# Posts' weights rounded on Pool, a fixed order at the end with the experts' sums in four stages, and a longer search for the order of the main loop

## The chip, the cores and the metric

The kernel runs on one core of one Trainium2 chip. The metric is the device time of one execution in microseconds; lower is better. The engines are named as in the profile: PE (TensorE; PEld its weight loads), DVE (VectorE), ACT (ScalarE), POOL (GpSimd), SP (SyncE, which issues all DMAs here).

## The reference

One transformer layer in float32 on 4 sequences of 2048 tokens with 256 channels.

```python
x = x + attn(layernorm(x))          # 16 heads of 16 channels, softmax over 2048 keys,
                                    # attn(y) = heads @ w_o.T + b_o + y
y = layernorm(x)
scores = softmax(y @ w_gate.T)      # 8 experts
s = (scores + expert_bias) in 4 groups of 2: keep the 2 groups with the largest sums
topk_idx = top 2 experts of what is kept; weights = scores there
flat_idx = topk_idx.reshape(-1)     # expert numbers, 0 to 7, are used as row numbers
routed_in = y[flat_idx] * weights   # so only rows 0 to 7 of y are ever gathered
counts = bincount(topk_idx)         # rows 0..counts[0]-1 go through expert 0, and so on
h = silu(grouped(routed_in, w1)) * grouped(routed_in, w3); routed_out = grouped(h, w2)
shared = silu(y @ sw1.T) * (y @ sw3.T) @ sw2.T
out = shared.at[flat_idx].add(routed_out)   # and only rows 0 to 7 of out receive them
x = x + out
```

## The kernel before, in words

**Chunks and units.** The tokens are cut into 16 chunks of 512. A chunk gets its layernorm, its projections to q, k and v (`qkv`, or hand-woven code for the first sequence), then attention, then its post work (`post`): output projection, second layernorm, transposes (`to_channels`), routing (`route`) and the shared feed-forward (`shared`, products `pa`, `pb`, `pd`). Attention runs in 64 units: one sequence, four heads and 512 queries each. Numbers are kept as a rounded high part and a low part (`h`, `l`), and a product is three matmuls (`mm3`).

**The three streams of a unit.** "M": a score matmul `mx` of 128 queries against 512 keys and a row maximum `ms` on DVE. "S": a score matmul `st` of 128 keys against 512 queries, with the maximum subtracted as a 64th row, and an exponential `et` on ACT. "A": the value matmuls `av`, eight PE instructions for four heads. The 4096 M, 4096 S and 1024 A of the whole run share seven PSUM banks (tags `b0` to `b6`). The maxima of a unit go through `mt` and a DMA into row 63 of its `qst` before its S may start.

**The order of the main loop.** The order is written out by the program itself while it is built, and the engines PE, DVE, POOL and ACT run it as written (`manual_schedule`). `Plan` books every instruction on model clocks. At each step `refill` puts up to `HORIZON` = 46 operations (M, S, A, the copy O of a finished unit, and P and D, pieces of side work) into a window, `Ahead.search` exchanges or moves two of them at random `TURNS` times and keeps an order by its modelled cost (simulated annealing), and the first `COMMIT` operations of the result are given out. Side work comes from generators; `need(kind, ns, *tiles)` says on which engine their next piece costs what and which tiles it waits for, `gate` holds one back until a condition holds. Pieces for ACT and POOL ("a", "p") are given out as soon as the plan thinks their tiles ready.

**Places the change touches.** `setup` loads w_o, s_1, s_3 and s_2 at the start of the third unit and splits each with `split(..., eng=G)`: the high part on ACT (`S.copy`), the low part on POOL. `post_first` loads a chunk's sums of exponentials and takes their reciprocals on DVE. After the last unit, `last_heads` finishes the last four heads, and `finish` runs two generators in turn for the last chunk: `front` (`post_a`, `route`, `moe`) and `behind` (`post_b`, the shared feed-forward). In `finish` the order on the engines is left to the framework's scheduler. `moe` builds one-hot tables for the 16384 routed rows, 16 groups of 1024: `ranges` (which expert a row falls to, from the counts `m_cum`), `pick` (one-hot `ob` on DVE, squared weights `ow` on POOL, then `mo` on PE and its copy `oT`), `hidden` (matmuls `mu`, sigmoid tables `mth` on ACT and DVE) and `gather` (matmuls into `pg`). In `pick` a group's `ob`, `mo` and `oT` stand together.

Of the kernel before, what the change touches and what calls it, by code (L numbers as in the profile page):

```python
# [32 lines left out]
LEAD0 = 3  # L33
LEAD = 6
HORIZON = 46
COMMIT = 10
LATE = 0.01, 0.1, 16
TURNS = 1600
WARM = 1.5
NET = 6  # L40
BANKS = 7
# [365 lines left out]
def body(tc, B, L, cols, x, wqkv, bqk, wst, bst, bv, wo, bo, wg, w1, w2, w3, sw1, sw2, sw3, ebias, cst, pad, out):  # L407
# [21 lines left out]
    def need(kind, ns=0, *tiles, more=0, act=940):  # L429


        return kind, ns, tiles, more, act

    def gate(open_):

        return "g", open_, (), 0, 0
# [43 lines left out]
    def split(name, tmp, out=None, eng=None):  # L480

        h, l = out or [cp.tile([P, 2, tmp.shape[2]], F32R, tag=f"{name}{q}", name=f"{name}{q}") for q in "hl"]
        S.copy(h, tmp)
        (eng or V).tensor_tensor(l, tmp, h.bitcast(F32), ALU.subtract)
        return h, l

# [73 lines left out]
    def to_channels(src, name, keep=None, fast=False, out=None):  # L560

        h, l = out or hl(f"t_{name}")
        if not fast:
            for c in range(2):
                f = keep[:, c, :] if keep is not None else sb.tile([P, QC], F32, tag="qkf", name=f"f_{name}{c}", bufs=2)
                pt = stile(f"pt_{name}{c}")
                for i in range(TQ):
                    T.transpose(pt[:, i * P:(i + 1) * P], src[:, i, c * P:(c + 1) * P], ident)
                S.copy(f, pt)
                G.tensor_copy(h[:, c, :], f)  # L570
                G.tensor_tensor(l[:, c, :], f, h[:, c, :].bitcast(F32), ALU.subtract)
                if c == 0:
                    yield need("s1", 436, act=470)
            return h, l
        for c in range(2):
            pt = mtile(f"pt_{name}{c}")
            for i in range(TQ):
                T.transpose(pt[:, i * P:(i + 1) * P], src[:, i, c * P:(c + 1) * P], ident)
            S.copy(keep[:, c, :], pt)
            S.copy(h[:, c, :], pt)  # L580
            V.tensor_tensor(l[:, c, :], pt, h[:, c, :].bitcast(F32), ALU.subtract)
            yield
        return h, l

    mark = {}
# [244 lines left out]
    def moe():  # L830
# [9 lines left out]
        V.tensor_copy(tot, pc[0:E, 0:P])  # L840
        cum = mtile("m_cum")
        T.matmul(cum[:, 0:E + 1], tot, K["below"][0:E, :], start=True, stop=True)
        ge = sb.tile([P, NR, E + 1], BF16, tag="vst", name="m_ge", bufs=2)
        oe = sb.tile([P, NR, E], BF16, tag="hq", name="m_oe", bufs=2)
        gb = sb.tile([P, E, 32], F32, tag="qkf", name="m_gb", bufs=2)
# [2 lines left out]
        pg = ps_av.tile([P, QC], F32, tag="av", name="pg")  # L848
        GR = 8
        NG = NR // GR  # L850
        ows, oTs, ths = {}, {}, {}

        def ranges(r0, r1):
            n = r1 - r0
            V.tensor_tensor(ge[:, r0:r1], K["rows"][:, r0:r1].unsqueeze(2).broadcast_to([P, n, E + 1]),
                            cum[:, 0:E + 1].unsqueeze(1).broadcast_to([P, n, E + 1]), ALU.is_ge)
            V.tensor_tensor(oe[:, r0:r1], ge[:, r0:r1, 0:E], ge[:, r0:r1, 1:E + 1], ALU.subtract)

        def pick(g):
            sl = slice(g * GR, (g + 1) * GR)  # L860
            ob = sb.tile([P, GR, E, 8], BF16, tag="x", name=f"ob_{g}", bufs=2)
            ow = ows[g] = sb.tile([P, GR, E, 8], F32, tag="lo", name=f"ow_{g}", bufs=3)
            ee = oe[:, sl, :].unsqueeze(3).broadcast_to([P, GR, E, 8])
            V.tensor_tensor(ob, ee, of[:, sl, :].unsqueeze(2).broadcast_to([P, GR, E, 8]), ALU.mult)
            G.tensor_tensor(ow, ee, oj[:, sl, :].unsqueeze(2).broadcast_to([P, GR, E, 8]), ALU.mult)
            pt = mtile(f"mo_{g}")
            obf = ob.rearrange("p r e j -> p (r e j)")
            for q in range(GR // 2):
                T.matmul(pt[:, q * P:(q + 1) * P], obf[:, q * P:(q + 1) * P], identb, start=True, stop=True)
            oT = oTs[g] = sb.tile([P, GR // 2, P], F32R, tag="hi", name=f"oT_{g}", bufs=3)  # L870
            V.tensor_copy(r2(oT), pt)
# [120 lines left out]
    last = {}  # L992

    def post_last():

# [67 lines left out]
            V.tensor_tensor(xv, pd, xv, ALU.add)  # L1063
        write(ch, x1)

    def post_b(ch, n, x1, x2T, x2hl, rt, eng=G, hhl=None):

        hT = f4(f"hT_{n}")
        hhl = hhl or hl(f"hT_{n}")
        for m in range(2):  # L1070
            pa = mtile(f"pa_{n}_{m}")
            mm3(pa, W["s_1"], x2hl, slice(m * P, (m + 1) * P), slice(0, QC))
            th = sb.tile([P, QC], F32, tag="sth", name=f"th_{n}_{m}", bufs=2)
            S.activation(th, pa, AF.Tanh, scale=0.5)
            if eng is G:
                yield
            if eng is None:
                S.copy(hT[:, m, :], pa)
                G.tensor_tensor(th, th, K["ones"][:, 0:1].broadcast_to([P, QC]), ALU.add)
                G.tensor_tensor(th, th, hT[:, m, :], ALU.mult)  # L1080
            else:
                V.scalar_tensor_tensor(th, th, 1.0, pa, ALU.add, ALU.mult)
            yield
            next(rt, None)
# [3 lines left out]
            if eng is None:  # L1088
                S.mul(hT[:, m, :], pb, 0.5)
                G.tensor_tensor(hT[:, m, :], hT[:, m, :], th, ALU.mult)  # L1090
            else:
                V.scalar_tensor_tensor(hT[:, m, :], pb, 0.5, th, ALU.mult, ALU.mult)
            S.copy(hhl[0][:, m, :], hT[:, m, :])
            (eng or G).tensor_tensor(hhl[1][:, m, :], hT[:, m, :], hhl[0][:, m, :].bitcast(F32), ALU.subtract)
            yield
            next(rt, None)
            yield
        yield
        for half in range(2):
# [24 lines left out]
    def finish():  # L1124
# [12 lines left out]
        while live:  # L1137
            for g in list(live):
                try:
                    next(g)  # L1140
                except StopIteration:
                    live.remove(g)


    queue, posts, side, norms, sums, firsts = (deque() for _ in range(6))
# [272 lines left out]
    def setup():  # L1418
# [359 lines left out]
```

## Time and profile before

| | |
|---|---|
| median of 3 runs | 3067.62 us (3067.2 to 3068.33) |
| the profiled execution | 3064.53 us, span 3062.7 us |
| mean granted PE clock | 0.986 |
| busy: PE, DVE, ACT, POOL | 2982.9, 2823.3, 2420.8, 649.9 us |
| first `st`, last `mx`, last `av` starts at | 93.5, 2930.5, 2970.3 us |
| row maxima `ms` | 4096, 682 ns each |
| exponentials `et` | 4096, 611 ns each |
| DMA | 237.32 MB, mean 77 GB/s |

All instructions carry line 56, that of the recording helper, so groups are told apart by tiles (`ms<-mx` is the row maximum of a score tile). The span is nearly all main loop; a busy PE is not PE at its peak, because ends of matmuls are modelled. In answers by stretch each line has the stretch, its length, the busy time of each engine with the number of instructions, the granted clock, the DMA share and GB/s. In a timeline each line has start and duration, and in brackets the idle time before it and what ended that.

### The profile page before, as it was taken

Reading aid. Unit: us, or ns where it says so; the run is one execution under the profiler, and the core shown is the slowest. Engines: PE = TensorE matmul, PEld = TensorE weight load, DVE = VectorE, ACT = ScalarE, POOL = GpSimd, SP = SyncE. Lnnn points to the kernel's source line nnn. Section 1 sums busy time; section 2 is a strip of 40 time slices with the busy share of each in tenths; the row PEclk is TensorE's granted clock in tenths of the full one; section 3 lists DMA queues with packets and bytes.
Section 4 is the critical chain, followed back from the end, with each engine's and each line's share of the span. In section 5 each row is a group of like instructions: output and inputs, shape, how many; then the busy total and the mean of one; then the engine's idle time right before and its main releaser. Section 6 shows DMA issues by size and latency. Waiting matters only on the chain.

```text
span 3062.7 us, 52745 instructions
## 1 busy us (share of the span) xinstructions
PE 2982.9 (97%) x19427; PEld 1359.8 (44%) x19427; DVE 2823.3 (92%) x5129; ACT 2420.8 (79%) x4745; POOL 649.9 (21%) x662
## 2 busy tenths in 40 slices
PE   7989999999999999999999999999999999999988
PEld 5434444444444444444444444444444444444436
DVE  7879999999999999999999999999999999999926
ACT  5578888888878878788888778888778788887774
POOL 5233223133213112110221220000222200023313
PEclk9899999999999999999999999999999999999998
DMA  5555645343121312221121200201121101011200
GB/s 157 184 156 151 167 114 162 94 140 112 51 94 40 115 32 88 64 79 69 44 86 39 72 25 20 90 22 69 45 75 49 69 25 58 31 54 40 77 26 15
DMA packets 144797, 237.32 MB, mean 77 GB/s; under 512 B 17115, under 2 KB 73563, under 8 KB 140379
## 3 DMA queue, kind: packets, MB, share of 16 engines
q1 hardware_dynamic: 144539, 233.96, 24.3%
q8 instruction: 153, 2.51, 0.3%
q14 instruction: 105, 0.86, 0.1%
HBM read 138.38 MB, written 111.80 MB: 82 GB/s over the span
## 4 chain that ended last, share of the span: by engine, by line
PE 80%; DVE 15%; DMA 1%; issue 1%; ACT 1%; POOL 1%; SPq 0%; POOLq 0%; ACTq 0%; DVEq 0%
PE av L56 29%; PE mx L56 20%; PE st L56 19%; DVE ms L56 11%; PE pp L56 3%; PE pd L56 2%; PE pv L56 1%; PE po L56 1%; PE pt_x L56 1%; PE pa L56 1%; PE pb L56 1%; PE mu L56 1%; ACT et L56 1%; PE pg L56 1%; DVE eq L56 1%
## 5 line engine op out<-in xcount | busy, mean ns | idle before, releaser
L56 DVE TENSOR_REDUCE ms<-mx 128x1 f32<-128x512 f32 x4096 | 2521.6, 682 | 135.0 <-PE mx L56 100.5
L56 ACT ACTIVATE et<-st 128x512 f32<-128x512 f32 x4096 | 2139.9, 611 | 440.4 <-PE st L56 288.2
L56 PE MATMUL mx<-kst,qst 63*128 63x512 f32 x3984 | 1222.7, 442 | 27.9 <-ACT et L56 10.6
L56 PE MATMUL st<-qst,kst 64*128 64x512 f32 x4032 | 1221.9, 440 | 7.3 <-DMA qst<-mt 3.4
L56 PE MATMUL av<-et,vst 128*32 128x512 f32 x8192 | 1098.4, 607 | 0.8 <-ACT ao L56 0.6
L56 PEld LDWEIGHTS mx<-kst,qst 63*128 63x128 f32 x3984 | 577.7, 186 | 605.8 <-DVE ms L56 289.8
L56 PEld LDWEIGHTS st<-qst,kst 64*128 64x128 f32 x4032 | 580.8, 186 | 556.1 <-DVE ms L56 278.9
L56 PEld LDWEIGHTS av<-et,vst 128*32 128x32 f32 x8192 | 164.0, 108 | 328.4 <-issue 307.7
L56 POOL TENSOR_TENSOR aT<-aT,rb 128x512 f32<-128x512 f32 (+1 forms) x32 | 40.9, 1285 | 571.3 <-DMA rb<-rd 570.9
L56 POOL CAST hi<-qkf 128x512 fp32r<-128x512 f32 x56 | 34.2, 610 | 328.3 <-ACT qkf L56 314.3
L56 POOL TENSOR_TENSOR lo<-qkf,hi 128x512 fp32r<-128x512 f32 x64 | 82.1, 1283 | 22.9 <-ACT hi L56 13.2
L56 ACT ACTIVATE qkf<-pp,b_qk 128x512 f32<-128x512 f32 x64 | 44.0, 687 | 53.8 <-PE pp L56 53.6
L56 POOL TENSOR_TENSOR th<-th,cs 128x512 f32<-128x512 f32 x32 | 33.5, 1046 | 222.8 <-ACT th L56 222.8
L56 POOL TENSOR_TENSOR rs_b<-rs_b,nhalf 128x4 f32<-128x4 f32 x16 | 16.3, 1017 | 279.7 <-DVE rs_b L56 279.7
L56 POOL TENSOR_TENSOR hT<-hT,th 128x512 f32<-128x512 f32 x32 | 41.0, 1281 | 123.7 <-ACT hT L56 47.4
L56 POOL TENSOR_TENSOR x<-x,xl 128x256 f32<-128x256 f32 x64 | 46.4, 755 | 16.8 <-ACT xl L56 16.8
L56 POOL TENSOR_TENSOR x<-x,b_o 128x256 f32<-128x256 f32 x64 | 45.5, 740 | 0.0
L56 ACT ACTIVATE xl<-x,rs_a 128x256 f32<-128x256 f32 x64 | 33.4, 594 | 11.1 <-DVE rs_a L56 11.0
L56 ACT COPY ao<-av 128x512 f32<-128x512 f32 x63 | 37.9, 601 | 3.0 <-PE av L56 2.0
L56 POOL TENSOR_TENSOR th<-th,sg 128x512 f32<-128x512 f32 x30 | 38.9, 1296 | 2.4
L56 ACT ACTIVATE th<-pa 128x512 f32<-128x512 f32 x32 | 19.2, 599 | 24.5 <-PE pa L56 24.2
L56 ACT ACTIVATE x<-x,rs_b 128x256 f32<-128x256 f32 x64 | 33.2, 597 | 6.6 <-DVE rs_b L56 6.6
(406 smaller groups left out, 2177.3 us busy)
## 6 DMA issues: line engine op xcount, KB each, us to landing
kst<-kd SPq DMA_DIRECT2D x16, 2048.0 KB
qst<-qd SPq DMA_DIRECT2D x63, 512.0 KB
qd<-hi SPq DMA_DIRECT2D x64, 256.0 KB
kd<-hi SPq DMA_DIRECT2D x64, 256.0 KB
ad<-ao SPq DMA_DIRECT2D x63, 256.0 KB
vst<-vd SPq DMA_DIRECT2D x19, 664.0 KB
vd<-vt SPq DMA_DIRECT2D x32, 332.0 KB
x<-x SPq DMA_DIRECT2D x16, 512.0 KB
```

The source lines that it names most:

```text
L56: r = f(*a, **k)
```

## The change

- `COMMIT` goes from 10 to 6 and `TURNS` from 1600 to 3600. Every choice of the search, and so the order of the whole main loop, comes out differently.
- A new gate `later(ns=12000)` holds a generator back until the plan's PE clock has gone on by 12 us. It stands behind each weight load in `setup` and behind the loads in `post_first`.
- With `eng=G`, `split` rounds the high part on POOL too.
- In the fast form of `to_channels` (last chunk) both copies `x2T` come first on ACT, then both rounded copies; the low parts are given out later, by `behind`.
- In `moe` the counts `m_cum` are copied to SBUF (`m_cm`) for `ranges`; `pick` is cut in two (`pick` and `turn`), so a group passes through four steps instead of three; `ow` has six buffers (tag `et`) instead of three.
- `post_b` does only matmuls and ACT copies first; its ten POOL operations are given out one per step once `moe` has reached its first group (`last["at"]`), and its `pd` matmuls after that.
- `finish` runs under `manual_schedule` for POOL, DVE, PE and ACT: instructions stay in the order in which the two generators give them out.

```diff
-COMMIT = 10
+COMMIT = 6
-TURNS = 1600
+TURNS = 3600
...
+    def later(ns=12000):
+        t = plan.clock["PE"] + ns
+        return gate(lambda: plan.clock["PE"] > t)
...
     def split(name, tmp, out=None, eng=None):
-        S.copy(h, tmp)
+        (S.copy if eng is None else eng.tensor_copy)(h, tmp)
         (eng or V).tensor_tensor(l, tmp, h.bitcast(F32), ALU.subtract)
...
+        pts = []
         for c in range(2):
-            pt = mtile(f"pt_{name}{c}")
+            pts.append(mtile(f"pt_{name}{c}"))
...
-            S.copy(keep[:, c, :], pt)
-            S.copy(h[:, c, :], pt)
-            V.tensor_tensor(l[:, c, :], pt, h[:, c, :].bitcast(F32), ALU.subtract)
-            yield
+            S.copy(keep[:, c, :], pts[c])
+        for c in range(2):
+            S.copy(h[:, c, :], pts[c])
+        def low():
+            for c in range(2):
+                V.tensor_tensor(l[:, c, :], pts[c], h[:, c, :].bitcast(F32), ALU.subtract)
+        last["low"] = low
+        yield
...
+        cm = sb.tile([P, E + 1], F32, tag="m_cm", name="m_cm", bufs=1)
+        V.tensor_copy(cm, cum[:, 0:E + 1])
...
-            ow = ows[g] = sb.tile([P, GR, E, 8], F32, tag="lo", name=f"ow_{g}", bufs=3)
+            ow = ows[g] = sb.tile([P, GR, E, 8], F32, tag="et", name=f"ow_{g}", bufs=6)
             V.tensor_tensor(ob, ee, ..., ALU.mult)
             G.tensor_tensor(ow, ee, ..., ALU.mult)
+        def turn(g):
             pt = mtile(f"mo_{g}")
...
-        for g in range(NG + 2):
+        for g in range(NG + 3):
+            last["at"] = g
             if g % STEP == 0 and g < NG:
                 ranges(g * GR, min(NR, (g + STEP) * GR))
+            if g >= 3:
+                gather(g - 3)
             if g < NG:
                 pick(g)
+            if 2 <= g < NG + 2:
+                hidden(g - 2)
             if 1 <= g <= NG:
-                hidden(g - 1)
-            if g >= 2:
-                gather(g - 2)
+                turn(g - 1)
...
+        yield later()                              # post_first, before the reciprocal
         yield need("d", 480, s1)
...
     def post_b(ch, n, x1, x2T, x2hl):              # was: products with POOL work between them
+        g2 = sb.tile([P, 2, QC], F32, tag="et", name=f"g2_{n}", bufs=6)
         for m in range(2):
             pa = mtile(f"pa_{n}_{m}")
             mm3(pa, W["s_1"], x2hl, slice(m * P, (m + 1) * P), slice(0, QC))
+            S.activation(ths[m], pa, AF.Tanh, scale=0.5)
+            S.copy(hT[:, m, :], pa)
             yield
             pb = mtile(f"pb_{n}_{m}")
             mm3(pb, W["s_3"], x2hl, slice(m * P, (m + 1) * P), slice(0, QC))
+            S.mul(g2[:, m, :], pb, 0.5)
+            yield
+        while last["at"] < 0:
+            yield
+        for m in range(2):
+            G.tensor_tensor(ths[m], ths[m], K["ones"][:, 0:1].broadcast_to([P, QC]), ALU.add)
+            yield
+            G.tensor_tensor(ths[m], ths[m], hT[:, m, :], ALU.mult)
+            yield
+            G.tensor_tensor(g2[:, m, :], g2[:, m, :], ths[m], ALU.mult)
+            yield
+            G.tensor_copy(hhl[0][:, m, :], g2[:, m, :])
+            yield
+            G.tensor_tensor(hhl[1][:, m, :], g2[:, m, :], hhl[0][:, m, :].bitcast(F32), ALU.subtract)
             yield
...
         def behind():
             while "q" not in last:
                 yield
-            yield from post_b(*last["q"], iter(()), None)
+            for _ in range(3):
+                yield
+            last["low"]()
+            yield
+            yield from post_b(*last["q"])
         live = [front(), behind()]
+        with tc.manual_schedule(engines={ENG.Pool, ENG.DVE, ENG.PE, ENG.Activation}):
...
             t = load_w(src, "sth", 2)
-            yield need("a", 530, t)
+            yield later()
+            yield need("p", 2600, t)
             W[n] = split(n, t, eng=G)
```

More of the change, by code (lines that the diff above doesn't have):

```diff
@@ L574, in to_channels @@
             return h, l
+        pts = []
         for c in range(2):
-            pt = mtile(f"pt_{name}{c}")
+            pts.append(mtile(f"pt_{name}{c}"))
             for i in range(TQ):
-                T.transpose(pt[:, i * P:(i + 1) * P], src[:, i, c * P:(c + 1) * P], ident)
-            S.copy(keep[:, c, :], pt)
-            S.copy(h[:, c, :], pt)
-            V.tensor_tensor(l[:, c, :], pt, h[:, c, :].bitcast(F32), ALU.subtract)
-            yield
+                T.transpose(pts[c][:, i * P:(i + 1) * P], src[:, i, c * P:(c + 1) * P], ident)
+            S.copy(keep[:, c, :], pts[c])
[6 more added lines that the diff above has]
+        yield
         return h, l
@@ L850, in moe @@
         NG = NR // GR
-        ows, oTs, ths = {}, {}, {}
+        obs, ows, oTs, ths = {}, {}, {}, {}
         def ranges(r0, r1):
@@ L855, in ranges @@
             V.tensor_tensor(ge[:, r0:r1], K["rows"][:, r0:r1].unsqueeze(2).broadcast_to([P, n, E + 1]),
-                            cum[:, 0:E + 1].unsqueeze(1).broadcast_to([P, n, E + 1]), ALU.is_ge)
+                            cm.unsqueeze(1).broadcast_to([P, n, E + 1]), ALU.is_ge)
             V.tensor_tensor(oe[:, r0:r1], ge[:, r0:r1, 0:E], ge[:, r0:r1, 1:E + 1], ALU.subtract)
@@ L860, in pick @@
             sl = slice(g * GR, (g + 1) * GR)
-            ob = sb.tile([P, GR, E, 8], BF16, tag="x", name=f"ob_{g}", bufs=2)
-            ow = ows[g] = sb.tile([P, GR, E, 8], F32, tag="lo", name=f"ow_{g}", bufs=3)
+            ob = obs[g] = sb.tile([P, GR, E, 8], BF16, tag="x", name=f"ob_{g}", bufs=2)
+            ow = ows[g] = sb.tile([P, GR, E, 8], F32, tag="et", name=f"ow_{g}", bufs=6)
             ee = oe[:, sl, :].unsqueeze(3).broadcast_to([P, GR, E, 8])
@@ L865, in pick @@
             G.tensor_tensor(ow, ee, oj[:, sl, :].unsqueeze(2).broadcast_to([P, GR, E, 8]), ALU.mult)
+        def turn(g):
             pt = mtile(f"mo_{g}")
-            obf = ob.rearrange("p r e j -> p (r e j)")
+            obf = obs.pop(g).rearrange("p r e j -> p (r e j)")
             for q in range(GR // 2):
@@ L990, in post_a @@
         return ch, n, x1, x2T, x2hl
-    last = {}
+    last = {"at": -1}
     def post_last():
@@ L1064, in shared, with post_b @@
         write(ch, x1)
-    def post_b(ch, n, x1, x2T, x2hl, rt, eng=G, hhl=None):
-        hT = f4(f"hT_{n}")
-        hhl = hhl or hl(f"hT_{n}")
+    def post_b(ch, n, x1, x2T, x2hl):
+        hT, hhl = f4(f"hT_{n}"), hl(f"hT_{n}")
+        g2 = sb.tile([P, 2, QC], F32, tag="et", name=f"g2_{n}", bufs=6)
+        ths = [sb.tile([P, QC], F32, tag="sth", name=f"th_{n}_{m}", bufs=2) for m in range(2)]
         for m in range(2):
@@ L1072, in post_b @@
             mm3(pa, W["s_1"], x2hl, slice(m * P, (m + 1) * P), slice(0, QC))
[L1073 to L1084, printed above, removed]
+            S.activation(ths[m], pa, AF.Tanh, scale=0.5)
+            S.copy(hT[:, m, :], pa)
             yield
@@ L1087, in post_b @@
             mm3(pb, W["s_3"], x2hl, slice(m * P, (m + 1) * P), slice(0, QC))
[L1088 to L1094, printed above, removed]
-            yield
-            next(rt, None)
+            S.mul(g2[:, m, :], pb, 0.5)
+            yield
+        while last["at"] < 0:
[10 more added lines that the diff above has]
+            G.tensor_tensor(hhl[1][:, m, :], g2[:, m, :], hhl[0][:, m, :].bitcast(F32), ALU.subtract)
             yield
@@ L1133, in behind @@
                 yield
-            yield from post_b(*last["q"], iter(()), None)
-        live = [front(), behind()]
[L1137 to L1142, printed above, removed]
+            for _ in range(3):
[3 more added lines that the diff above has]
+            yield from post_b(*last["q"])
+        live = [front(), behind()]
+        with tc.manual_schedule(engines={ENG.Pool, ENG.DVE, ENG.PE, ENG.Activation}):
+            while live:
+                for g in list(live):
+                    try:
+                        next(g)
+                    except StopIteration:
+                        live.remove(g)
     queue, posts, side, norms, sums, firsts = (deque() for _ in range(6))
```

## The prediction

> **What bounds the kernel now.** I read the page first (shares, slices, chain), then one answer with the busy time of every stage, then the timeline at the worst stall and at the end. The page says that TensorE is never idle, but ends of matmuls are modelled, so I do not take that as the bound:
>
> ```profile
> PE 2982.9 (97%) x19427; PEld 1359.8 (44%) x19427; DVE 2823.3 (92%) x5129; ACT 2420.8 (79%) x4745; POOL 649.9 (21%) x662
> PE 80%; DVE 15%; DMA 1%; issue 1%; ACT 1%; POOL 1%; SPq 0%; POOLq 0%; ACTq 0%; DVEq 0%
> L56 DVE TENSOR_REDUCE ms<-mx 128x1 f32<-128x512 f32 x4096 | 2521.6, 682 | 135.0 <-PE mx L56 100.5
> ```
>
> One row maximum shows 682 ns, but back to back they start 0.60 us apart (the chain has "DVE ms x14" in 8.45 us). 4096 x 0.60 = 2458 us of 3062.7: VectorE is the engine that must not starve in the main loop, and TensorE decides whether it does. The stages:
>
> ```profile
> core 0: us, PE busy (x) PEld busy (x) DVE busy (x) ACT busy (x) POOL busy (x), PEclk, DMA share, GB/s
> 93.50:213.00 119.50, 113.93 (x680) 51.52 (x678) 104.06 (x185) 89.22 (x171) 30.78 (x36) 0.95 0.50 157
> 213.00:222.00 9.00, 0.12 (x1) 0.00 (x0) 1.81 (x3) 1.98 (x4) 2.21 (x2) 0.62 0.79 303
> 222.00:230.00 8.00, 7.78 (x32) 2.73 (x33) 3.56 (x7) 4.00 (x9) 4.36 (x5) 0.58 0.34 95
> 230.00:2931.00 2701.00, 2681.01 (x17623) 1188.80 (x17621) 2582.81 (x4688) 2204.66 (x4307) 527.41 (x526) 1.00 0.23 73
> 2931.00:2971.00 40.00, 36.59 (x206) 12.12 (x205) 1.68 (x4) 32.62 (x66) 6.18 (x6) 0.91 0.11 35
> 2981.50:3007.70 26.20, 19.67 (x78) 12.74 (x78) 15.49 (x32) 9.62 (x18) 10.38 (x10) 0.64 0.06 21
> 3007.70:3056.70 49.00, 43.45 (x448) 35.65 (x448) 36.43 (x58) 27.58 (x80) 17.66 (x16) 0.93 0.04 12
> ```
>
> To see: in the loop (93.5 to 2931, 2837.5 us) VectorE is busy 104.06 + 1.81 + 3.56 + 2582.81 = 2692 us, so all that any order can win is 145 us, and 12 of them lie in two lines, 213 to 230. The last 40 us of exponentials (0.49 us each) are bound by ScalarE and not touched. The end after 2981.5 is 81 us, and the change rewrites its order.
>
> All sums are made on the profiled execution: 3064.53 us (span 3062.7 and 1.8 around it). The median of the runs, 3067.62, is 3.1 us above it; I subtract the same microseconds from it.
>
> **The posts' weights on Pool.** The stall at 213 us, in three engines' rows and the queue's:
>
> ```profile
> 207.70 1.20 SPq L56 DMA_DIRECT2D kst<-kd  x1
> 209.91 5.24 SPq L56 DMA_DIRECT2D wt<-sw  x2
> 220.35 0.62 ACT L56 CAST s_3h<-wt 128x512 fp32r<-128x512 f32 x1 [6.94 <-DMA wt<-sw]
> 222.22 0.79 PE L56 MATMUL mx<-kst,qst 63*128 63x512 f32 x1 [9.09 <-ACT et L56]
> 223.05 0.69 DVE L56 TENSOR_REDUCE ms<-mx 128x1 f32<-128x512 f32 x1 [8.23 <-PE mx L56]
> ```
>
> The two weight loads stand in the queue behind a 2 MB key load; ScalarE, in its fixed order, waits 6.94 us for one with the exponentials behind it, so banks stay full, TensorE stops 9.09 us and VectorE 8.23. Then the granted clock is 0.58 until 230, and VectorE is busy 3.56 of 8 us where the loop's average is 2583/2701 = 96%: 4.1 us more. The changed program has the four roundings on Pool and each load a `later()` gate before its use; nothing on ScalarE then waits for these loads. Gain 8.2 + 4.1 = 12.3, and four roundings of 0.62 leave ScalarE (2.5 us, not the bound: nothing). I take **12**, bounds 8 (the clock falls anyway, for another reason) and 14. Pool receives four casts (0.61 each); if a load is late, Pool waits and behind it stand the next `hi`/`lo`, their stores on SP and the unit's `qst` load. Cover: Pool is busy 4.36 of 8 us here and 21% overall. If that cover is gone, the nearest row is TensorE's wait for `qst<-qd` at 128.3, 4.16 us.
>
> **The order of the loop.** The built orders say what the search did. From first score to last value matmul there were 2552 runs of TensorE work of one kind and are now 2532: value groups 1039 to 1031, score and maximum runs 1268 to 1255. Runs of 12 or more rise from 56 to 81, runs of 3 or less from 32 to 53. Pricing every run by the mean that its kind and length took in the trace (6 score matmuls 0.98 us, 12 of them 2.65, a value group 1.01, a projection of 6 at 512 columns 1.61) gives 2877 before, which is the stage itself, and 2879 after, two unseen lengths being put in at 2.8 together. Second reading: cut both orders at every value group, price VectorE (0.60 a maximum), ScalarE (0.49 an exponential) and TensorE (unstalled runs) in each piece and add the largest: 2863 before and 2858 after; with two groups in a piece 2748 and 2752, with four 2701 and 2710. So the order as such is within -5 to +10 of the old one; what such sums don't see is the 145 us of fine stalls, of which a better search may take some. I take **4** gained, bounds -12 (lost) and 25 (a sixth of 145). The `later()` gates in `post_first` cost nothing: the only wait of a reciprocal is the last (7.1 us for `s<-ad` at 2932), whose chain ends on Pool at 2953.4, 18 us before its reader.
>
> **The end: routing.** Here Pool's post work stands in VectorE's way:
>
> ```profile
> 2992.57 1.23 DVE L56 TENSOR_TENSOR sel<-sc,e_b 128x32 f32<-128x32 f32 x1
> 2998.24 1.20 DVE L56 TENSOR_TENSOR k<-k,kn 128x32 f32<-128x32 f32 x1
> 2992.47 1.29 POOL L56 TENSOR_TENSOR th<-th,hT 128x512 f32<-128x512 f32 x1
> ```
>
> `sel` ends when Pool's multiply ends; in the routing at 2890 us the same operation took 0.19. Seven of them are stretched (sel, gt, kp, kn, k, gt, gt): 1.04 + 0.95 + 0.49 + 1.07 + 1.01 + 1.01 + 0.98 = 6.5 us, all on the path. The new order lets Pool start only after the first `ow`, so these 6.5 go. The router's matmuls, now mixed with pa and pb, end at 2989.35; alone, after `x2T`'s second copy (one copy earlier), they end near 2985.7: 3.6 gained. The two low halves (1.35 on VectorE) fit under the exponential (1.75 in the trace): 0.4. m_tot and m_cum no longer stand among pd and its adds: 1.0 after paying the copy `cm` (0.25). Sum 11.5. Against it: pa and pb, 24 matmuls, now stand ahead of m_pc; at 0.23 they end near when it is due, at the 0.43 of the slow clock up to 4 later. I take **10**, bounds 7 and 11.5.
>
> **The end: experts in four stages.** In its steady state a group takes 2.35 us with TensorE full (pg 1.03, mo 0.21, mu 1.1):
>
> ```profile
> 3033.39:3035.74 2.35, 2.35 (x29) 2.04 (x28) 1.99 (x4) 1.80 (x7) 1.06 (x1) 1.00 0.00 0
> ```
>
> Before, ranges to m_sg took 49.0. After: lead-in to the first pg (ranges 0.8, ob 0.7, mo 0.5, oT 0.7, mu 1.9 at the slow clock, sigmoids 2.3) 6.9; 14 groups x 2.35 = 32.9; last two 4.8; two pd blocks 24 x 0.115 = 2.8; a slow clock at the start as in before, 2. That is 49.4. Pool now has two operations in ten steps (1.05 + about 1.1 of 2.35), and `ob` meets them. Low end: the steady rows, where ob is 0.78 against 0.68, so nothing; high end: the two ob at 3008.90, 1.5 each with Pool full, which makes VectorE's 2.0 to 2.8 and the step 0.5 longer, 5. I take 3 because Pool will be nearly full. So 52.4: **3.4 lost**, bounds 1 gained and 8 lost.
>
> The Trainium skill, "SBUF — State Buffer", section "Who interferes with whom", speaks against this step: a vector operation with two SBUF inputs and a Pool operation that reads SBUF exclude each other for a whole instruction. By it each of the ten ob could wait a whole Pool operation, an estimate of 8 us for the stage; the steady row (0.78 with ow running) says that most do not.
>
> **Sum.** 12 + 4 + 10 - 3.4 = 22.6, say 23: 3041.5 for a profiled execution, 3044.6 for the median.
>
> **Rivals.** (1) The search pays more than the run counts show: 25 in place of 4. For it: 3.75 times as many exchanges for each operation given out, and longer runs; against: the priced orders are equal. 3067.6 - 44 = 3024. (2) The gains don't add: the new order has three more `qd` stores ahead of the third unit's `qst` load, so the 4.16 us stall at 128 grows by as much and the slow clock after it lasts longer (8 in all), the order costs 8 and the experts' stage 5: -12 + 8 + 8 - 10 + 5 = -1, so 3067. (3) Slower: the uneven order starves VectorE. Long runs fill the seven banks and value groups come late; short ones leave turns. Its price is the idle share of the loop: each tenth of 145 is 14.5. It must eat the 19 of the other steps and 6 more, 25 us, or 17% more idle, to be slower; at a third more it costs 48: 3097 at most, 3078 at its middle. The four-group sum (+10) speaks for it, the one-group sum (-5) and fewer turns against. (4) The change does what it says for the weights only, the end being bound by TensorE anyway: 3052, inside my range.
>
> **Numbers.** Forecast with (4) 0.61, rival 1 0.15, rival 2 0.13, rival 3 0.11. This kernel's measurement can tell about 0.2%, 6.1 us, from no change: below 3061.5 lie the forecast, rival 1 (0.76), within it rival 2 (0.13), above rival 3 (0.11). The range goes from rival 1's end to rival 2's: 3022 to 3067.
>
> **What would show it.** No ScalarE wait for `wt` near 200 to 240 us and no TensorE gap of 9 us there; `sel`, `k`, `gt` of the last routing at 0.2 to 0.4; lgT done before pa; m_ge some 10 us after pt_x sooner; groups at 2.35 to 2.9; last exponential about 16 us earlier. It is wrong if VectorE's idle time between first score and last maximum is above 145, or if the experts' stage takes over 57 us.

## Result and profile after

The changed kernel takes 3091.65 us (3089.38 to 3092.01, 3 runs) against 3067.62: ratio 1.0078, 95% interval 1.0064 to 1.0091. It is slower by 24 us where 23 gained were forecast. Its profiled execution has a span of 3089.8 us, 27.1 above before's. The page of after, the lines that answer to those of before:

```profile
PE 2991.4 (97%) x19427; PEld 1363.9 (44%) x19427; DVE 2830.2 (92%) x5130; ACT 2418.0 (78%) x4739; POOL 658.3 (21%) x668
L56 DVE TENSOR_REDUCE ms<-mx 128x1 f32<-128x512 f32 x4096 | 2518.1, 681 | 148.1 <-PE mx L56 108.4
```

The row maxima are unchanged (2518.1 against 2521.6 us), yet VectorE as a whole is busy 6.9 us longer: its other operations got longer. The page alone does not say where. Busy time by stretch does: first the loop of before (first score to last row maximum), then after's loop, the first wait, the place of the old weights' stall, the last routing and the experts' stage.

```profile
93.10:2931.70 2838.60, 2803.89 (x18340) 1243.72 (x18341) 2692.65 (x4882) 2300.22 (x4488) 564.77 (x568) 0.99 0.25 77
```

```profile
core 0: us, PE busy (x) PEld busy (x) DVE busy (x) ACT busy (x) POOL busy (x), PEclk, DMA share, GB/s
95.50:2954.70 2859.20, 2809.71 (x18338) 1244.51 (x18338) 2701.83 (x4879) 2297.50 (x4484) 568.06 (x571) 0.99 0.24 77
129.00:139.00 10.00, 0.37 (x4) 0.08 (x1) 1.03 (x3) 2.00 (x4) 3.75 (x4) 0.75 0.60 223
200.00:240.00 40.00, 39.33 (x258) 17.83 (x250) 35.56 (x66) 33.92 (x68) 17.04 (x22) 1.00 0.67 196
3006.90:3022.30 15.40, 13.83 (x54) 8.88 (x54) 7.78 (x32) 7.17 (x14) 0.75 (x3) 0.63 0.10 34
3022.30:3083.80 61.50, 53.86 (x472) 42.69 (x472) 38.15 (x59) 29.44 (x81) 31.39 (x26) 0.92 0.03 10
```

The 27 us are made up so: the start 2.4 later, the loop 2859.2 against 2838.6 (20.6 lost), the last value groups 0.9 lost, and the end from the last value matmul on 3.1 lost. Inside the loop, VectorE's idle time went from 146 to 157 us (stretch less busy time), and its busy time grew by 9 although it has the same operations (862 besides the row maxima in both). Inside the end, routing (first transpose `pt_x` to `m_ge`) fell from 25.95 to 15.35 us, and the experts' stage (`m_ge` to `m_sg`) rose from 48.95 to 61.49.

**The weights' stall is gone, another wait has grown.** From 200 to 240 us TensorE is busy 39.33 of 40 at full clock. Measured by the first value matmul of each unit, after is 8.4 us behind before at unit 2 and 5.6 ahead at unit 3: 14.0 gained in between. But it had lost 8.9 by unit 1. The timeline of after there, SP's issues and TensorE:

```profile
126.19 0.66 SPq L56 DMA_DIRECT2D qd<-lo  x1
...
128.63 0.93 SPq L56 DMA_DIRECT2D qst<-qd  x1
...
137.63 3.03 SPq L56 DMA_DIRECT2D qst<-mt  x3
138.95 0.76 PE L56 MATMUL mx<-kst,qst 63*128 63x512 f32 x1 [9.63 <-DMA qst<-qd]
```

The `qst` load is issued behind the stores at 128.63, where before had it at 121.79; TensorE's wait for it is 9.63 us in place of 4.16.

**What the loop loses later** comes bit by bit (by unit 17 after is still 9 ahead, at unit 62 it is 27 behind). Three of the five largest steps from one unit to the next (46 to 47, 60 to 61 and 61 to 62, 5 to 7 us each) hold a gap like the one here, in after's timeline:

```profile
2210.62 2.40 POOL L56 TENSOR_TENSOR hT_0l<-hT,hT_0h 128x1024 fp32r<-128x1024 f32 x1
...
2210.85 2.45 DVE L56 TENSOR_TENSOR eq<-eq,cs 128x256 f32<-128x256 f32 x1
2213.22 0.68 DVE L56 TENSOR_REDUCE ms<-mx 128x1 f32<-128x512 f32 x1
...
2213.96 0.79 PE L56 MATMUL mx<-kst,qst 63*128 63x512 f32 x1 [2.73 <-DVE ms L56]
```

A routing operation of VectorE that takes 0.42 us elsewhere (as at 3016.80 in after) lasts 2.45 and ends 0.28 us behind Pool's 2.40 us subtraction. Behind it a row maximum waits, its bank stays taken, and TensorE stands 2.73 us for it. The granted clock is at half for 6.8 us, from 2212.7 on: one score matmul takes 0.79 where those just before the gap took 0.50 and less. After has four such gaps of TensorE in the loop (2.74, 2.73, 3.29 and 2.21 us, at 1692, 2211, 2825 and 2890), each with a VectorE operation held by a Pool operation ahead of it.

### The profile page after: what moved, and what is told of

Its sections match the earlier page's. It is cut to its first block, busy times and chain, and to the rows that moved or that the text cites. A ratio compares the mean times of both kernels' runs of the same rounds, so it can differ in the third digit from the quotient of the medians.

```text
span 3089.8 us, 52819 instructions
## 1 busy us (share of the span) xinstructions
PE 2991.4 (97%) x19427; PEld 1363.9 (44%) x19427; DVE 2830.2 (92%) x5130; ACT 2418.0 (78%) x4739; POOL 658.3 (21%) x668
## 4 chain that ended last, share of the span: by engine, by line
PE 79%; DVE 16%; DMA 2%; ACT 1%; issue 1%; POOL 1%; SPq 0%; POOLq 0%; ACTq 0%; DVEq 0%
PE av L56 28%; PE mx L56 20%; PE st L56 19%; DVE ms L56 10%; PE pp L56 3%; PE pd L56 2%; PE pv L56 1%; PE po L56 1%; PE pt_x L56 1%; PE pb L56 1%; PE pa L56 1%; DVE eq L56 1%; DMA qd<-lo 1%; DVE gt L56 1%; ACT et L56 1%
## 5 line engine op out<-in xcount | busy, mean ns | idle before, releaser
L56 DVE TENSOR_REDUCE ms<-mx 128x1 f32<-128x512 f32 x4096 | 2518.1, 681 | 148.1 <-PE mx L56 108.4
L56 PE MATMUL st<-qst,kst 64*128 64x512 f32 x4032 | 1219.0, 441 | 27.1 <-DVE ms L56 17.2
L56 POOL TENSOR_TENSOR aT<-aT,rb 128x512 f32<-128x512 f32 (+1 forms) x32 | 40.7, 1283 | 645.5 <-DMA rb<-rd 645.2
L56 ACT ACTIVATE qkf<-pp,b_qk 128x512 f32<-128x512 f32 x64 | 44.0, 688 | 48.8 <-PE pp L56 48.5
L56 POOL TENSOR_TENSOR rs_b<-rs_b,nhalf 128x4 f32<-128x4 f32 x16 | 16.3, 1020 | 260.3 <-DVE rs_b L56 260.3
```

What stands on the lines that cost most here:

```text
L56: r = f(*a, **k)
```

## Experiments

Three sums are used for every loop. "Idle" is the loop's length less VectorE's busy time in it. "Held" is, over all VectorE operations in the loop but the row maxima, the time of each above the shortest of the same operation and shape. "Half clock" is the time at half granted clock in spells that begin after 240 us (within the loop). The sums are made from single records and may differ by 0.5 from a stretch row. Loop less idle less held is 2649 to 2655 us in all of them, as it must be for the same operations, so idle and held time carry the differences between loops; this alone says nothing of a cause. Every VectorE operation of the loop that lost more than 0.2 us had a Pool operation beside it: 39 of them with 33 us in before, 47 with 42 us in after.

Each loop is read from one execution. Before's order, traced again in b_tail and b_tail5, has loops of 2841.0 and 2840.2 us, and after's order in a_gather one of 2856.4; so a difference of 3 us between two loops tells nothing.

| kernel | time, us | ratio to before, 95% | loop | idle | held | half clock |
|---|---|---|---|---|---|---|
| before | 3067.6 | 1 | 2838.6 | 146 | 40 | 10 |
| after | 3091.7 | 1.0064 to 1.0091 | 2859.2 | 157 | 48 | 37 |
| a_cut | 3075.2 | 1.0018 to 1.0037 | 2842.9 | 152 | 37 | 20 |
| b_cut | 3057.5 | 0.9955 to 0.9978 | 2830.0 | 147 | 31 | 3 |
| b_cut128 | 3066.4 | 0.9993 to 1.0012 | 2829.1 | 151 | 28 | 3 |
| b_seed2 | 3094.0 | 1.0065 to 1.0095 | 2863.3 | 167 | 45 | 24 |
| b_seed3 | 3081.5 | 1.0027 to 1.0054 | 2852.5 | 160 | 40 | 24 |
| b_search | 3086.7 | 1.0029 to 1.0061 | 2859.0 | 157 | 50 | 31 |
| b_search2 | 3086.6 | 1.0051 to 1.0084 | 2857.9 | 163 | 41 | 27 |
| b_search3 | 3080.2 | 1.0025 to 1.0054 | 2850.0 | 156 | 39 | 21 |
| a_oldsearch | 3077.7 | 1.0016 to 1.0037 | 2845.9 | 150 | 41 | 14 |
| a_seed2 | 3079.5 | 1.0024 to 1.0053 | 2849.9 | 152 | 43 | 37 |
| b_best | 3042.9 | 0.9901 to 0.9931 | 2827.4 | 146 | 32 | 3 |

Names in a_ start from the changed kernel, names in b_ from the kernel before. Before itself had medians of 3067.8 to 3070.2 on the chips of these runs.

### Pool's operations in pieces: a_cut and b_cut

The first theory: the loop loses because routing operations of VectorE are held for the whole of the Pool operation that is running. Every plain two-dimensional Pool copy or two-input operation of more than 256 columns is given out in pieces of 256 (the weights' and the experts' `ow` stay whole); the plan still books it as one, so the order of the loop stays as it was, in a_cut after's and in b_cut before's.

```diff
-                r = f(*a, **k)
+                if self.cut and name in ("tensor_tensor", "tensor_copy") and n > 256 ...:   # Pool only
+                    for c in range(0, n, 256):
+                        r = f(*(x[:, c:c + 256] if hasattr(x, "tensor") else x for x in a), **k)
+                else:
+                    r = f(*a, **k)
```

> The changed kernel in the same order, with every Pool copy or product wider than 256 columns issued as pieces of 256. Theory of the port: in the main loop VectorE's small routing operations are held until a Pool operation ends (48 us in all, single ones 1 to 2.4 us), TensorE runs dry and its clock falls; pieces take 0.75 us at most, so the held time falls to 20 to 30 us, the TensorE gaps above 2 us at 1692, 2211, 2825 and 2889 go, and the total falls by 10 to 20, to 3072 to 3082. Rival: the order itself is worse, not what meets on the port; then the total stays within 4 of 3091, or rises because Pool has more instructions.

> The kernel before in its own order, with every Pool copy or product wider than 256 columns issued as pieces of 256, as in a_cut. Theory of the port: 40 us of VectorE's time in the loop and 6.5 us in the last routing are held by Pool here; cut in pieces they fall to about half, total 3047 to 3060. Rival (the port does not matter in the loop): within 4 of 3067.

a_cut: 3075.18 us, 16 less than the changed kernel with its order; b_cut: 3057.45, 10.9 less than before on the same chip. One group of VectorE operations in the groups' view of before, after and a_cut in turn (count, busy us, mean ns):

```profile
L56 DVE TENSOR_SCALAR kn<-kp 128x16 f32<-128x16 f32 x16 | 3.8, 235 | 0.0
```

```profile
L56 DVE TENSOR_SCALAR kn<-kp 128x16 f32<-128x16 f32 x16 | 8.1, 507 | 0.0
```

```profile
L62 DVE TENSOR_SCALAR kn<-kp 128x16 f32<-128x16 f32 x16 | 5.2, 323 | 0.0
```

The same 16 operations average 235 ns in before and 507 in after (507 again in a_gather, which has after's order), and 323 with pieces in after's order; unheld, one takes 160. In before's order this group is no evidence: it averages 235 ns in before, 167 in b_tail with the same order, and 196 with pieces. In after's order the pieces take 12 us of held and 5 of idle time away, which is the loop's 16.3; in before's order 10 of held time, and the loop falls 8.6. The order of the loop is untouched, so the length of Pool's operations is shown as the cause of that much. It is not all of after's loss: a_cut's loop is still 13 above b_cut's.

Three parts of the expectations missed. Held time fell to 37 us in a_cut and not to 20 to 30. Of the four gaps of TensorE three went, but one of 2.57 us stayed at 1688. In b_cut the last routing did not get shorter (26.7 us against 25.95), although its held time fell from 6.8 to 5.1.

### Smaller pieces: b_cut128

```diff
-                if self.cut and name in (...) and n > 256 ...:
+                if self.cut and name in (...) and n > 128 ...:      # pieces of 128
```

> Before's order with Pool's operations in pieces of 128 columns in place of 256. Theory (a VectorE operation waits for the Pool piece that is running, so its hold halves with the piece): held time of the routing operations in the loop falls from 31 us at 256 to 22 to 27 (uncut 40), time 3051 to 3057. Rival (the gain of the pieces comes from spreading Pool's work, or Pool's fixed cost for each piece eats it): same as at 256 or slower, 3057 to 3064.

3066.44 us: the rival has the total. The loop is as good as b_cut's (2829.1; held 28 against 31, not the 22 to 27 expected), but the first `st` starts 4.3 us later (99.0 against 94.8) and the end from the start of the last value matmul is 4.3 longer (97.1 against 92.8; the routing takes 28.5 against 26.7, the experts' stage 51.3 against 48.8). That nothing hides Pool's longer work in these two places is argued, not shown. One group of Pool operations (64 of 1283 ns in before) shows the price, in b_cut and in b_cut128:

```profile
L60 POOL TENSOR_TENSOR lo<-qkf,hi 128x256 fp32r<-128x256 f32 x128 | 91.3, 735 | 16.7 <-ACT hi L62 16.0 <-POOL lo L60 0.7
```

```profile
L60 POOL TENSOR_TENSOR lo<-qkf,hi 128x128 fp32r<-128x128 f32 x256 | 109.9, 465 | 14.5 <-ACT hi L62 9.6 <-DMA kd<-lo 4.5 <-POOL lo L60 0.4
```

1283, 735 and 465 ns for 512, 256 and 128 columns are about 0.19 us for each instruction and 2.14 ns for each column. Pool as a whole works 659 us in before, 760 with pieces of 256 and 976 with pieces of 128 (the sum of its operations).

### The order as a draw: b_search, b_seed2, b_seed3, a_oldsearch

The second theory: the search's orders differ in idle and held time by chance, since its costs know neither the hold nor the clock, and the order of before is a lucky one. b_search is before with the new `COMMIT` and `TURNS` alone; b_seed2 and b_seed3 are before with other random numbers alone; a_oldsearch is the changed kernel with the old two constants.

```diff
-COMMIT = 10
+COMMIT = 6                      # b_search; the reverse in a_oldsearch
-TURNS = 1600
+TURNS = 3600
...
-        self.random = Random(1).random
+        self.random = Random(2).random      # b_seed2; 3 in b_seed3
```

> The kernel before with the search's settings alone changed (six operations given out, 3600 exchanges); posts, weights and end are as before. Theory (the order is blind to the port that VectorE and Pool share, so each order draws its own number of held operations and of short slow clocks): between 3056 and 3082, the loop (first score to last row maximum) within 15 us of before's 2837 either way, and the loop's change follows its half-clock time (before 10 us after 240 us, after 37). Rival (these settings themselves make a worse order): 3080 to 3095, the loop 12 to 27 us longer. Rival (they make a better one, and the changed kernel's loss comes from the gated posts): 3040 to 3060.

> The kernel before with another seed of the search's random numbers and nothing else: same settings, same work, another order. Theory (luck of the order is as large as the loop's loss): differs from 3068 by 4 to 15 us, either way. Rival (the order's quality is set by the settings): within 3 us of 3068.

> As the second seed: a third drawing of the same settings. Theory: the three seeds spread over 8 to 25 us. Rival: all within 4 us.

> The changed kernel with the old settings of the search (ten given out, 1600 exchanges). The end stays as in after (3 us longer than before's), the weights' stall stays away. Theory (luck): 3060 to 3090, no direction. Rival (the new settings cost the loop 24 us): 3064 to 3072, since the loop loses its 24 and keeps the weights' gain.

All four are slower than before, by 7.5 to 24 us. One changed seed, nothing else, costs 24 us, as much as the whole change under study; its loop in the stretch view has 167 us of idle VectorE:

```profile
96.40:2959.70 2863.30, 2818.00 (x18339) 1241.84 (x18339) 2695.90 (x4880) 2297.68 (x4488) 565.11 (x568) 0.99 0.24 77
```

a_oldsearch missed the 3064 to 3072 of "the new settings cost the loop 24". The theory missed too, by being too mild: b_seed2 lies 24 us off where 4 to 15 were expected, and b_search's 3086.7, with a loop 20 longer, lies outside its 3056 to 3082 and inside the rival's "these settings themselves make a worse order". The next runs are for that rival.

### Settings or luck: b_search2, b_search3, a_seed2

The two seeds again, with the new settings, and the changed kernel with the second seed.

> The kernel before with the new settings of the search and the second seed. The three old-setting orders have loops of 2838.6, 2863.3 and 2852.5 us (mean 2851.5), the one new-setting order 2859.0. Theory (settings do not matter, the order is a draw): loop anywhere from 2838 to 2866, time 3068 to 3096. Rival (the new settings draw worse): loop over 2862, time over 3090.

> As before this, third seed. Theory: the mean of the three new-setting loops lies within 8 us of 2851.5. Rival (new settings worse): mean above 2860. Rival (new settings better, before's own order being a lucky one): mean below 2843.

> The changed kernel with the second seed. Its end is after's (93 to 96 us from the last value matmul), its loop a new draw. Theory: between 3070 and 3095, the weights' stall at 213 absent. Rival (the changed kernel's loop is bad because of the gates, not by luck): 3088 to 3096.

The loops of before's program are 2838.6, 2863.3 and 2852.5 at the old settings (mean 2851.5) and 2859.0, 2857.9 and 2850.0 at the new (mean 2855.6). The means differ by 4, inside the 8 that the theory allowed: neither a worse nor a better search shows at this number of draws. The three loops with the gates (2859.2, 2845.9, 2849.9; mean 2851.7) are no worse than the rest, and a_seed2's 3079.5 lies below the 3088 to 3096 of "bad because of the gates". Of nine orders before's is the shortest, by 7 us to the next (5 with its repeats) and 18 to the mean of the five redraws without gates.

### The weights alone: b_weights

Before with the four roundings on Pool, without the gate, in before's order.

```diff
-        S.copy(h, tmp)
+        (S.copy if eng is None else eng.tensor_copy)(h, tmp)
```

> The kernel before in its own order, with only the four roundings of the posts' weights issued on Pool in place of ScalarE (the order is planned as if they were still on ScalarE). Theory: the 9.09 us stop of TensorE at 213 and the slow clock after it go, 12 us, total 3055 to 3057. Rival: something else on the path fills the gap (the key load's traffic, Pool waiting for the load with the next projection's parts behind it); then the gain is under 5 us.

3068.03 us, ratio 0.9995 (0.9984 to 1.0006): nothing gained. The timeline of b_weights shows where the wait went:

```profile
221.17 0.61 POOL L486 CAST s_3h<-wt 128x512 fp32r<-128x512 f32 x1 [4.96 <-DMA wt<-sw]
...
224.98 1.02 POOL L56 TENSOR_TENSOR rs_a<-rs_a,nhalf 128x4 f32<-128x4 f32 x1
226.03 0.55 DVE L56 SCALAR_TENSOR_TENSOR rs_a<-mv_a,rs_a 128x4 f32<-128x4 f32 x1 [7.71 <-POOL rs_a L56]
...
227.24 0.79 PE L56 MATMUL mx<-kst,qst 63*128 63x512 f32 x1 [7.13 <-DVE ms L56]
```

Pool now waits for `wt`, with a layernorm's `rs_a` behind it; VectorE, in its fixed order, waits 7.71 us for `rs_a`, and TensorE 7.13 for VectorE. So the roundings on Pool do not take the stall away by themselves. With the gate as well it is gone in all three orders that have both: after, a_oldsearch and a_seed2 have no gap of TensorE above 1.4 us from 140 to 1480 us, where before and its five redraws each have one of 4.6 to 18.2 us at the weights, between 205 and 240. No run has the gate with the roundings left on ScalarE, so whether the gate alone would do is not shown.

### The end alone: b_tail

Before with the changed end (`to_channels`, `moe`, `post_b`, `finish`) and nothing else; its loop is before's order.

> The kernel before with the changed end alone (routing and experts in the fixed order of four stages); the order of the main loop is before's, instruction for instruction. Theory (the end gives 10.6 in the routing and takes 12.5 in the experts' stage): 3068 to 3072, m_ge to m_sg 60 to 64 us, groups at 3.3. Rival (the experts' stage was slow in the changed kernel for a reason of that run, such as the clock): 3058 to 3063, stage 50 to 54.

3070.24 us, ratio 1.0009 (1.0000 to 1.0018); routing 15.2 us, experts 61.4. The end gives 11 and takes 12, whatever the loop does.

### Gather behind hidden: a_gather

Why is a step of the experts' stage 3.31 us in after? The late steps, with no post work left on Pool, in after's timeline:

```profile
3069.82 0.66 PE L56 MATMUL pg<-mth,ow 128*64 128x128 f32 x8 [0.25 <-ACT mth L56]
...
3070.41 0.39 PE L56 MATMUL mu<-ah,oT 128*128 128x256 f32 x1
...
3071.72 0.69 DVE L56 TENSOR_TENSOR mth<-mu,wgt 128x512 f32<-128x512 f32 x1 [1.42 <-POOL ow L56]
...
3072.45 0.63 ACT L56 ACTIVATE mth<-mth 128x512 f32<-128x512 f32 x1
...
3073.13 0.66 PE L56 MATMUL pg<-mth,ow 128*64 128x128 f32 x8 [0.25 <-ACT mth L56]
...
3075.03 0.69 DVE L56 TENSOR_TENSOR mth<-mu,wgt 128x512 f32<-128x512 f32 x1 [1.43 <-PE mu L56]
```

It is a closed chain: the second half of `pg` waits for the sigmoid, `mu` stands behind `pg` on TensorE, `mth` waits for the last `mu`, the sigmoid for `mth`, and the next `pg` for the sigmoid: 3069.82 to 3073.13. (The first `mth` shown is put down to the last `ow`, which ended just then; the next one, with no `ow` left, starts as long after its `mu` and is put down to that.) The first attempt to open it puts `gather` behind `hidden`.

```diff
-            if g >= 3:
-                gather(g - 3)
...
             if 2 <= g < NG + 2:
                 hidden(g - 2)
+            if g >= 3:
+                gather(g - 3)
             if 1 <= g <= NG:
                 turn(g - 1)
```

> The changed kernel, with gather(g - 3) moved behind hidden(g - 2) in the loop over groups; everything before the last 70 us keeps its order. Theory: with pg ahead of mu on TensorE, a step is a closed chain (mu, the multiply mth on VectorE, the sigmoid on ScalarE, pg, next mu), which is the 3.31 us per group of the changed kernel; with mu between them the step falls to 2.35 to 2.6 us, the stage from ranges to m_sg from 61.5 to 47 to 51 us, and the total to about 3079. Rival: Pool's post operations, which meet VectorE's one-hot products, make the stage long; then it stays above 57 us and the total within 3 of 3091.

3091.04 us, no gain: the expectation failed, and the stage takes 63.9 us. The rival, Pool's post work, named such numbers, but it is not the cause of a late step, where that work is done and a step still takes 3.35 us. Another chain closes:

```profile
3068.44 0.69 DVE L56 CAST oT<-mo 128x512 fp32r<-128x512 f32 x1 [0.40 <-PE mo L56]
...
3069.18 0.39 PE L56 MATMUL mu<-ah,oT 128*128 128x256 f32 x1 [0.78 <-DVE oT L56]
```

`mo` is now the last of a step, so the next step's first product, `mu`, waits for its copy `oT`.

### Five stages: b_tail5

The base is b_tail, before's loop with the changed end. Every product gets a whole step between the making of its input and its use: `pg` of group g-4, then `mo` of g-1, then `mu` of g-2; `ow` is made with `mu`, so that it lives three steps.

```diff
-        for g in range(NG + 3):
+        for g in range(NG + 4):
-            if g >= 3:
-                gather(g - 3)
+            if g >= 4:
+                gather(g - 4)
             if g < NG:
                 pick(g)                 # ob alone
-            if 2 <= g < NG + 2:
-                hidden(g - 2)
             if 1 <= g <= NG:
                 turn(g - 1)
+            if 2 <= g < NG + 2:
+                weigh(g - 2)            # ow, three buffers of tag lo
+                hidden(g - 2)
```

> As the changed end alone, but with five stages in the order ob(g), mo(g-1), mu(g-2), and pg of g-4 ahead of them, so that every product has one whole step between its input's making and its use; ow is made with mu and kept in three buffers. Theory (the four-stage order closes a chain mu, sigmoid table, sigmoid, pg, next mu inside one step): groups at 2.35 to 2.6, m_ge to m_sg 48 to 53, 3057 to 3062. Rival (Pool's post operations between the ow set the step): 2.8 to 3.3 in the ten steps with post work and 2.35 only in the last five, stage 55 to 60, 3063 to 3068.

3056.44 us, ratio 0.9963 (0.9948 to 0.9978); `m_ge` to `m_sg` 48.3 us. A late step in the stretch view of b_tail5:

```profile
3038.34:3040.68 2.34, 2.34 (x32) 2.04 (x28) 1.97 (x4) 1.76 (x5) 1.13 (x1) 1.00 0.14 43
```

TensorE is full again at 2.34 us a step. Pool's post work still lies between the `ow`; the rival that it sets the step gave 55 to 60 for the stage. By `oT`, the first step takes 1.7, five with that work 2.5 to 3.0 and one 4.5, then three take 1.8 to 2.1: the spare step lets TensorE catch up. One of 5.2 holds the `pd` products. So Pool's work lengthens single steps, but it does not set the stage.

### The best version: b_best

Before's loop order, Pool's operations in pieces of 256, and the end in five stages.

> Before's loop order, Pool's operations in pieces of 256 columns, and the end in five stages. Theory (the two gains are in different places and add): 3044 to 3050. Rival (cutting Pool's operations had most of its gain in the end, where the new order holds them away from the routing already): 3051 to 3056.

3042.89 us (3041.70 to 3043.25), ratio 0.9916 (0.9901 to 0.9931): 25 us under before, 49 under the changed kernel. The gains add, b_cut's 10.9 and b_tail5's 11.4 to 24.9. The loop of b_best in the stretch view (its experts' stage is 46.8 us):

```profile
94.20:2921.60 2827.40, 2799.85 (x18338) 1244.06 (x18339) 2680.85 (x4880) 2299.32 (x4488) 625.53 (x1057) 1.00 0.25 78
```

## Why the prediction was wrong, point by point

**Weights and gate: right.** 12 forecast, bounds 8 and 14; 14.0 between the units 2 and 3. Of the two reasons given, the roundings on Pool are not enough: b_weights has them and gains nothing, so the gate is needed. The paragraph on Pool's queue named the next `hi` and `lo` as what stands behind a late load; the one that hurt in b_weights was `rs_a`, for which VectorE waits.

**The order of the loop: the step that failed.** 4 gained was forecast, with 12 lost as the bad bound. The loop lost 20.6 with the 14.0 of the weights in it, so the order cost about 35 (a difference of two measured sums, not a measurement by itself). Of that 3 to 6 is the longer wait for `qst<-qd` at 129 (9.6 in after and 10.7 in a_gather, 4.2 to 7.0 in before, b_tail and b_tail5). Two things were missing. First, the sums priced every operation at the trace's mean, so they could not see an operation held by Pool; I read seven held operations in the routing at 2990 and used the same row to price the end only, although the other routings run in the loop beside the same Pool operations. Held time is 8 us more in after, and pieces of 256 columns take 12 of it and 5 of idle time away. Second, the range of the term came from before's own order, as if a new order were a small step from it. The five redraws without gates have loops 11 to 25 us longer than before's, and that is the range that this term should have had. After's loop, 20.6 longer, lies inside it; its 35 is no like figure, because each redraw still has a stall of its own at the weights. The count of runs and the piecewise sums, which said "equal", had no power to tell such orders apart.

**Rival 3** (the order starves VectorE; must eat 25 us) is nearest in sign and size: idle time rose from 146 to 157 although the 8.2 of the weights' stall went out of it, and the sign of being wrong, more than 145, came true (though before itself has 146 by this reading). It had 0.11. The mechanism given, seven banks filled by long runs, is not shown by any run. **Rival 2's** mechanism was right: the `qst` load behind more stores, 4.16 to 9.63 us; its sum of 3067 was not, because the order cost 35 and not 8. **Rival 1** (a better search) is not seen in the six orders of before's program at two settings. **Rival 4** fell with the routing's gain.

**Routing: right.** 10 forecast, 10.6 measured (and 10.8 in b_tail); `sel`, `k` and `gt` take 0.19, 0.19 and 0.42. Its two main terms hold one by one: the time that VectorE operations are held there fell from 6.8 to 0.2 us (6.5 forecast), and from the first `pt_x` to the first use of `lgT` on VectorE it takes 4.2 in place of 7.6 us (3.6 forecast). The delay behind `pa` and `pb` is there too (`m_tot` waits 2.19):

```profile
3013.66 0.19 DVE L56 TENSOR_TENSOR sel<-sc,e_b 128x32 f32<-128x32 f32 x1
...
3021.32 0.28 DVE L56 COPY m_tot<-m_pc 8x128 f32<-8x128 f32 x1 [2.19 <-PE m_pc L56]
```

**Experts' stage: the second step that failed.** 3.4 lost was forecast with 8 as the bound (its high end of 5 on 49.4 makes 5.4); 12.5 were lost, and the stage is over the 57 named. The failing term is "14 groups x 2.35": that row came from before, where the framework's order was `pg`, `mo`, `mu` with longer distances, and was carried over to a hand-written order without following one group round its step. Walking it (`pg` half 0.6, eight `mu` 1.2, `mth` 0.7, sigmoid 0.6, and the hand-overs) gives the 3.3 that after shows; 14 groups at 0.96 more are 13.4 us, the size of what was lost. The Trainium skill, "SBUF — State Buffer", section "Who interferes with whom", was weighed here and not in the loop. Here it did not decide: the step is 3.31 with Pool's post work done and 3.31 to 3.32 in three steps with it, and b_tail5 has that work and 48.3 us. In the loop it told: by the page a VectorE operation with two SBUF inputs and a Pool operation that reads SBUF exclude each other for a whole instruction, and after's `eq<-eq,cs` of 0.42 us lasted 2.45 beside a Pool subtraction of 2.40. The trace agrees with the page there.

**What stays open.** Which feature of an order sets its idle time, which spans 146 to 167 us over the nine orders. Half clock goes with it only loosely: 10 us with 146, 24 with 167, but 37 with 152. That the hold and the short gaps of TensorE behind it contribute is shown by the pieces; the rest is not.

## What to carry to other kernels

When a change makes a random search or a scheduler draw a new order, its price is the spread of such draws, and other seeds, nothing else changed, measure it; the current order may be the lucky end of it. A VectorE operation beside a long Pool operation is priced by the Pool operation's length, and one cure is to cut Pool's work into pieces, down to where its fixed cost (0.19 us here) shows on a path that nothing hides. In a hand-written software pipeline follow one item round one step on all engines: a period carried over from another order says nothing, and a chain that closes inside a step was opened here by one more stage, while the one other order of the same stages that was tried closed another chain.

## What was not expected of the hardware

- A VectorE operation with a single tensor input is held too, and for as long: `kn<-kp` (0.16 us alone) lasted 2.32 beside a Pool subtraction of 2.38, and `kp<-rk` (0.17) 0.76 beside a Pool cast. Both names stood among the prediction's seven; it did not carry them into the loop.
- In after four TensorE gaps of 2.2 to 3.3 us in a loop that is otherwise full each came with 3.4 to 6.8 us of half granted clock, with score matmuls at 0.79 in place of 0.50 us. No least gap can be read from this: before's gaps of 1.6 and 1.7 us (at 1818 and 2837) came with 3.4 us too, one of 2.2 in b_seed2 (at 2208) with none, and after has two spells of 3.4 (at 888 and 1591) with no gap above 1 us beside them.
- Halving the pieces again (128 columns) hardly lowers the held time, 31 to 28 us, where going from 512 and 1024 columns to 256 took 10.
